# Another order of the convolution units, norms of q and k spread through DRAM, and part of the last depthwise convolution on TensorE

## The chip, the cores and the metric

The kernel runs on one core of a Trainium2 chip: TensorE (PE), VectorE (DVE), ScalarE (ACT), GpSimd (POOL) and SyncE (SP), each with its own in-order instruction stream, and the DMA engines that they feed. The time is the device time of one execution in microseconds; a kernel's time is the median of its runs. All data are float32.

## The reference

The model has three layers: attention behind a hybrid of convolutions, a two-way state-space layer (mamba), and a mixture of experts. Only the first one bears on the change:

```python
x = x + conv_attn(_gn(x), W1, W3, W5, Wdw, Wproj, temperature)     # 1 x 64 x 64 x 256

def conv_attn(x, ...):
    qkv = concat([conv(xc, W1, 0), conv(xc, W3, 1), conv(xc, W5, 2)])   # q: 1x1, k: 3x3, v: 5x5
    qkv = conv(qkv, Wdw, 1, groups=3 * c)                               # 3x3 depthwise
    q, k, v = split(qkv)                  # 8 heads of 32 channels, 4096 pixels
    q, k = l2n(q), l2n(k)                 # t / max(sqrt(sum(t * t)), 1e-12)
    attn = softmax(einsum(q, k) * temperature)
    return conv(einsum(attn, v), Wproj, 0)
```

So q comes of a 1x1 convolution, k of a 3x3 and v of a 5x5 one, each followed by a depthwise 3x3 convolution; q and k are then divided by their norms over the 32 channels of a head.

## The kernel before

**Layout.** Channels lie on the 128 partitions, in two tiles of channels (t = 0, 1), pixels along the free axis. The image is worked in two halves of rows (half = 0, 1). One *unit* is a kind, a half and a tile, such as v10: kind v, half 1, tile 0. There are twelve: first k00, k01, k10, k11, then q00, v00, q10, v01, q01, v10, q11, v11.

**Products.** The convolutions k and v run as a Winograd scheme along the width. `weights` makes transformed weights on DVE (from raw weights that POOL loads into `wr`) and stores them to DRAM through POOL (`uk`, `uv`); SP loads them back as `u`. `inputs` makes the transformed image `v` from `xpad` on DVE. A unit of k has six products, one of v eight; each is a chain of matmuls of PE into one PSUM bank (`cv`, line 452, ten for v and six for k). A unit of q has four short products straight from `xpad` (line 444). `feed` (depth 3) issues products up to three ahead of those that DVE has taken, in the order of `units`; `product` hands out the next one.

**Main part of a unit.** `transform_out` takes the products in pairs: ACT copies one of a pair out of PSUM (`c`, L481), DVE adds and subtracts (L275, `out_t`) and sums into a padded image `pad` (L272); `sides` (ACT, L504 and L505) writes the two side columns. For q, `evacuate` lets ACT copy the four products into `pad`.

**Depthwise part.** `depthwise` makes tap 0 on ACT (L524) for two blocks, then the other eight taps of each on DVE (L528), 128x1280 elements a tap in half 1 and 128x768 in half 0. It is a generator and runs a unit late: the taps of one unit are stepped beside the main part of the next. For v, `turn` then transposes 128x128 blocks on PE (L587), copies them on ACT (L589) and stores them to `vd` through POOL (L590).

**Norms.** For q and k the rows go onto `rows_left` in chunks of 512 pixels; a *round* takes three. `norm_sums` squares on ACT (L550) and sums over a head on PE into `ps` (L551), the sum standing on eight rows a head, 32 a chunk. `norm_inverse` takes the maximum on DVE (L558), the root on ACT (L559) and the reciprocal on DVE (L560) of 96x512, then spreads it to all channels on PE (L565). `norm_apply` multiplies on DVE (L275, `acc`), puts q into another order on ACT (L574) and stores to `qd` or `kd` through POOL (L578). Each of the three is started one tick after the one before, from the list `events`; `tick` is called once a group.

**Order.** The engines' order is the program's (a schedule written out by hand). The loop over the units runs `groups` times per unit: 3 for k, 4 for v, 1 for q. In each group it steps the main part, calls `feed` and `tick`, steps the depthwise part of the unit before (18 steps over the groups), then does `share[kind]` steps of the filler work (`step_fill`: weights and inputs of later units), and feeds again.

```python
for g in range(groups):
    step(main)
    feed()
    tick()
    for _ in range(-(-18 // groups)):
        step(before)
    for _ in range(share[kind]):
        step_fill()
    feed()
```

**Hand-over.** After the last unit, `before` (the taps of v11) is drained, and then the events that are left. `Early` loads weights of the next layer (`win`, `wx`, `wdt`) on SP's queue and makes the diagonals `taps` on DVE (L802) in its constructor; then the attention phase loads `wpj`, the first `q`, and `kS` and `vT` for both tiles (`load_kv`), before its first scores (L954) and exponentials (L961).

Of the kernel before, what the change touches and what calls it, by code (L numbers as in the profile page):

```python
# [14 lines left out]
FP = mybir.dt.float32  # L15
# [9 lines left out]
P = 128  # L25
# [148 lines left out]
def conv_phase(cx, xT, w1, w3, w5, temp, qd, kd, vd, uk, uv):  # L174
# [17 lines left out]
    with ExitStack() as ctx:  # L192
# [56 lines left out]
        for t in range(CT):  # L249
            x = tp.tile([P, 4, 32], FP, name="px", tag="t")  # L250
            nc.vector.tensor_scalar(
                x, heads[:, None, :].to_broadcast([P, 4, 32]), temp[:, t : t + 1], None, ALU.mult
            )
            y = one.tile([P, 4, 32], FP, name=f"px{t}")
            nc.vector.tensor_tensor(y, x, first_of[:, None, :].to_broadcast([P, 4, 32]), ALU.mult)
            ps = pms.tile([P, N], FP, name="ps", tag=f"ps{t}")
            nc.tensor.transpose(ps[:, 0:P], y.rearrange("p a b -> p (a b)"), cx.ident)
            pq = one.tile([P, P], FP, name=f"pick_q{t}")
            nc.vector.tensor_copy(pq, ps[:, 0:P])
            pick_q.append(pq)  # L260
# [149 lines left out]


        units = [("k", h, t) for h in range(2) for t in range(CT)]
        for i in range(4):
            units += [("q", i % 2, i // 2), ("v", i // 2, i % 2)]
        jobs = [
            (u, i) for u in units for i in (range(4) if u[0] == "q" else PTS[u[0]])
        ]
# [85 lines left out]
        def sides(pad, r0):  # L503
            nc.scalar.copy(pad[:, r0 : r0 + HR, 0, 1:TX], pad[:, r0 : r0 + HR, 4, 0 : TX - 1])  # L504
            nc.scalar.copy(pad[:, r0 : r0 + HR, 5, 0 : TX - 1], pad[:, r0 : r0 + HR, 1, 1:TX])  # L505

        def depthwise(kind, half, t, pad):

            row0, n = (LAG, H - LAG) if half else (0, LAG)
            ch = {"q": 0, "k": CT, "v": 2 * CT}[kind] + t  # L510
            dst = accp.tile([P, (H - LAG) * W], FP, name="acc", tag="acc")

            def piece(b, tap):
                dy, dx = divmod(tap, 3)
                m = n // 2
                return (
                    dst[:, m * W * b : m * W * (b + 1)].rearrange("p (h w) -> p h w", w=W),
                    pad[:, m * b + dy : m * b + dy + m, dx : dx + 4, :].rearrange("p h s j -> p h (s j)"),
                    wdw[:, 9 * ch + tap : 9 * ch + tap + 1],
                )  # L520

            for b in range(2):
                o, src, w_ap = piece(b, 0)
                nc.scalar.activation(o, src, AF.Copy, scale=w_ap)  # L524
            for b in range(2):
                for tap in range(1, 9):
                    o, src, w_ap = piece(b, tap)
                    nc.vector.scalar_tensor_tensor(o, src, w_ap, o, ALU.mult, ALU.add)  # L528
                    yield
                if kind == "v":  # L530
                    turn(dst, t, row0 * W // P, n * W // P // 2 * b, n * W // P // 2)
            if kind != "v":
                c0 = row0 // ROWS
                rows_left.extend((dst[:, N * j : N * j + N], kind, t, c0 + j) for j in range(n // ROWS))
                if not busy:
                    norm_sums()

        def norm_sums():  # L540

            chunks = rows_left[:3]
            del rows_left[:3]
            busy[:] = chunks
            if not chunks:
                return
            ps = pms.tile([P, N], FP, name="ps", tag="ps0")
            for j, (a, _, _, _) in enumerate(chunks):
                sq = tp.tile([P, N], FP, name="sq", tag="t")
                nc.scalar.activation(sq, a, AF.Square)  # L550
                nc.tensor.matmul(ps[32 * j : 32 * j + 32, :], heads, sq, start=True, stop=True)  # L551
            later(lambda: norm_inverse(chunks, ps))

        def norm_inverse(chunks, ps):

            n = 32 * len(chunks)
            rn = rp.tile([P, N], FP, name="rn", tag="rn")
            nc.vector.tensor_scalar(rn[0:n, :], ps[0:n, :], 1e-24, None, ALU.max)  # L558
            nc.scalar.activation(rn[0:n, :], rn[0:n, :], AF.Sqrt)  # L559
            nc.vector.reciprocal(rn[0:n, :], rn[0:n, :])  # L560
            back = []
            for j, (_, kind, t, _) in enumerate(chunks):
                back.append(pms.tile([P, N], FP, name="ps", tag=f"ps{j}"))
                r = slice(32 * j, 32 * j + 32)
                nc.tensor.matmul(back[j], (pick_q[t] if kind == "q" else pick)[r, :], rn[r, :], start=True, stop=True)  # L565
            later(lambda: norm_apply(chunks, back))

        def norm_apply(chunks, back):
            for (a, kind, t, c), ps in zip(chunks, back):
                plus(a, a, ps, ALU.mult)  # L570
                if kind == "q":

                    s = tp.tile([P, N], FP, name="qo", tag="t")
                    nc.scalar.copy(  # L574
                        s.rearrange("p (h j r) -> p h r j", j=TX, r=4), a.rearrange("p (h r j) -> p h r j", r=4, j=TX)
                    )
                    a = s
                nc.gpsimd.dma_start(out=(qd if kind == "q" else kd)[t][:, N * c : N * c + N], in_=a)  # L578
            norm_sums()
# [25 lines left out]
        with tc.manual_schedule(engines=ORDERED):  # L605
# [85 lines left out]
                return False  # L691


            share = {"k": 5, "q": 4, "v": 3}
            before = None
            for n, (kind, half, t) in enumerate(units):
                pad, r0 = pads[n % 2], 9 if half else 1
                edge = edges["q" if kind == "q" else t]
                if half:
                    nc.scalar.copy(pad[:, 0:9], edge)  # L700
                    nc.gpsimd.memset(pad[:, HR + 9, :, :], 0.0)
                else:
                    nc.gpsimd.memset(pad[:, 0, :, :], 0.0)
                if kind == "q":
                    def evacuate():
                        for i in range(4):
                            r = r0 + 16 * (i // 2)
                            nc.scalar.copy(
                                pad[:, r : r + 16, 1 + 2 * (i % 2) : 3 + 2 * (i % 2), :],
                                product().rearrange("p (h s j) -> p h s j", s=2, j=TX),  # L710
                            )
                        sides(pad, r0)
                        yield

                    main, groups = evacuate(), 1
                else:
                    main, groups = transform_out(kind, pad, r0), len(PTS[kind]) // 2
                for g in range(groups):
                    step(main)
                    feed()  # L720
                    tick()
                    for _ in range(-(-18 // groups)):
                        step(before)
                    for _ in range(share[kind]):
                        step_fill()
                    feed()
                drain(main)
                drain(before)
                if not half:
                    nc.scalar.copy(edge, pad[:, LAG : LAG + 9])  # L730
                before = depthwise(kind, half, t, pad)
            drain(before)
            while events:
                tick()
# [5 lines left out]
class Early:  # L740
# [3 lines left out]
    def __init__(self, cx, pool, w_in, w_x, w_dt):  # L744
        nc = self.nc = cx.nc
        self.cx, self.pool = cx, pool
        self.win = pool.tile([P, CT, 2 * DI], FP, name="win0")
        nc.sync.dma_start(out=self.win, in_=w_in[0])
        self.wx = pool.tile([P, ET, DR + 2 * DS], FP, name="wx0")
        nc.sync.dma_start(out=self.wx, in_=w_x[0])  # L750

        self.wdt = pool.tile([32 + DR, DI], FP, name="wdt")
        for d in range(2):
            nc.sync.dma_start(out=self.wdt[32 * d : 32 * d + DR, :], in_=w_dt[d])
        self.taps = pool.tile([P, ET * 4, P], FP, name="taps0")
        diagonals(cx, self.taps, 0)

    def new_u(self):
        return self.pool.tile([P, CT, N], FP, name="u", tag="u")
# [53 lines left out]
def attention_phase(cx, early, xT, wproj, qd, kd, vd, x1d, ud):  # L813
# [8 lines left out]
    with ExitStack() as ctx:  # L822
# [10 lines left out]
        kS = one.tile([P, CT, NT], FP, name="kS")  # L833
        vT = one.tile([P, NB, C], FP, name="vT")
        wpj = tl.tile([P, CT, C], FP, name="wpj")
        nc.sync.dma_start(out=wpj, in_=wproj)
        ones = tl.tile([P, 32], FP, name="ones")
        nc.vector.memset(ones, 1.0)

# [98 lines left out]

        last, due, turning, queue = None, None, [], []
        q_next = load_q(0)  # L940
        for t in range(CT):
            load_kv(t)
        for c in range(NCH):
            q_t = q_next
            if c + 1 < NCH:
# [1050 lines left out]
def kernel(  # L1996
# [55 lines left out]
    with tc.If(nc.values_load(beyond[0:1, 0:1]) > 0):  # L2052
        general_attention_phase(cx, xT, wproj, over, qd, qg, kd, vd, md, x1g, ug)
        with tc.tile_pool(name="early", bufs=1) as pool:
            early = Early(cx, pool, w_in, w_x, w_dt)
            with tc.tile_pool(name="g_psx", bufs=2, space=PSUM) as psx:
                drain(early.stage(ug, lambda: psx.tile([P, 2, N], FP, name="sx", tag="sx")))
            mamba_phase(cx, early, w_in, w_x, w_out, w_m1, w_m2, x1g, ug, bcg, dtg, x2g, u2g, usum)
# [93 lines left out]
```

## Time and profile before

| what | us |
|---|---|
| median of 3 runs (lowest, highest) | 4239.93 (4239.77, 4242.26) |
| the profiled execution, its time | 4233.11 |
| its span | 4231.3 |
| PE busy (share of the span) | 3603.2 (85%) |
| DVE busy | 3503.0 (83%) |
| ACT busy | 2675.6 (63%) |
| POOL busy | 1740.9 (41%) |
| granted clock of PE, mean | 0.918 |
| last `pad` of the last unit starts | 635.97 |
| first matmul of the scores | 703.54 |
| first exponential | 706.98 |
| PE busy in the attention, 703.5 to 1990 | 1269.96 of 1286.50 |

The profile is of one execution, and times in it are from the start of its span. A group of instructions is named by its line, its engine and its tiles, written as output<-inputs; the number in brackets behind a row is the idle time of the engine before it and what ended it. "x12" is twelve instructions or records; a float32 matmul of this kernel leaves two records.

### The profile page before, as it was taken

Reading aid. Unit: us, or ns where it says so; the run is one execution under the profiler, and the core shown is the slowest. Engines: PE = TensorE matmul, PEld = TensorE weight load, DVE = VectorE, ACT = ScalarE, POOL = GpSimd, SP = SyncE. Lnnn points to the kernel's source line nnn. Section 1 sums busy time; section 2 is a strip of 40 time slices with the busy share of each in tenths; the row PEclk is TensorE's granted clock in tenths of the full one; section 3 lists DMA queues with packets and bytes.
Section 4 is the critical chain, followed back from the end, with each engine's and each line's share of the span. In section 5 each row is a group of like instructions: output and inputs, shape, how many; then the busy total and the mean of one; then the engine's idle time right before and its main releaser. Section 6 shows DMA issues by size and latency. Waiting matters only on the chain. (4 is left out here: it accounts for less than half of the span.)

```text
span 4231.3 us, 43479 instructions
## 1 busy us (share of the span) xinstructions
PE 3603.2 (85%) x15080; PEld 1175.6 (28%) x15080; DVE 3503.0 (83%) x2898; ACT 2675.6 (63%) x4176; POOL 1740.9 (41%) x1132
## 2 busy tenths in 40 slices
PE   4769894999999999999788888878888888875798
PEld 2324341222222222222222222222222222321343
DVE  6997876888888888778899999999999999999211
ACT  1111224888788788777777778777787777774122
POOL 2210000000000000000888889888888888897000
PEclk9889996999999999999888999989899898977899
DMA  4422224000000000002333443433334433432121
GB/s 160 138 77 92 75 75 133 4 28 15 21 26 11 24 24 15 17 14 74 115 125 113 130 117 123 126 115 123 115 108 125 130 124 116 133 117 73 65 65 39
DMA packets 150531, 351.18 MB, mean 83 GB/s; under 512 B 35493, under 2 KB 44453, under 8 KB 150046
## 3 DMA queue, kind: packets, MB, share of 16 engines
q1 hardware_dynamic: 139214, 313.17, 23.4%
q0 software_dynamic: 11088, 35.14, 2.4%
q8 instruction: 120, 1.97, 0.2%
q14 instruction: 109, 0.89, 0.1%
HBM read 268.69 MB, written 79.56 MB: 82 GB/s over the span
## 5 line engine op out<-in xcount | busy, mean ns | idle before, releaser
L1677 POOL TENSOR_TENSOR dbx<-dtxr,b 128x1024 f32<-128x1024 f32 x512 | 1203.0, 2361 | 201.9 <-DVE da L1688 106.0
L961 ACT ACTIVATE e<-sc 128x1024 f32<-128x1024 f32 x1024 | 992.6, 1023 | 201.4 <-PE sc L954 160.3
L1688 DVE TENSOR_TENSOR_SCAN da<-da,state,dbx 128x1024 f32<-128x1024 f32 x432 | 1014.3, 2348 | 40.4 <-ACT state L1716 19.3
L882 DVE TENSOR_TENSOR s<-s,e 128x1024 f32<-128x1024 f32 x768 | 880.8, 1218 | 45.4 <-ACT e L961 44.9
L1667 ACT ACTIVATE da<-dtr,aneg 128x512 f32<-128x512 f32 x1024 | 708.0, 691 | 32.8 <-DMA dtr<-dtd 2.9
L954 PE MATMUL sc<-q,kS 32*128 32x512 f32 x4096 | 653.6, 643 | 19.5 <-DMA kS<-kd 13.0
L132 POOL TENSOR_TENSOR ln_few<-ln_few,minus_half 128x4 f32<-128x4 f32 x29 | 29.5, 1016 | 1414.2 <-DMA ln_few<-ln_row 1414.2
L1693 DVE TENSOR_TENSOR h<-da,c 128x1024 f32<-128x1024 f32 x432 | 529.2, 1225 | 32.6 <-DVE da L1688 0.4
L889 PE MATMUL av<-e,vT 128*32 128x512 f32 x4096 | 548.9, 607 | 3.7 <-ACT o L895 3.7
L452 PE MATMUL cv<-v,u 128*128 128x512 f32 x928 | 420.7, 614 | 58.8 <-DVE pad L272 21.2
L1725 PE MATMUL y<-h,sel 128*32 128x512 f32 x2048 | 378.7, 655 | 101.3 <-DVE h L1693 83.9
L954 PEld LDWEIGHTS sc<-q,kS 32*128 32x128 f32 x4096 | 211.6, 183 | 465.5 <-issue 244.3
L1251 PE MATMUL mm<-u,win 128*128 128x512 f32 x496 | 255.4, 663 | 80.9 <-ACT z L1362 34.3
L452 PEld LDWEIGHTS cv<-v,u 128*128 128x128 f32 x928 | 181.1, 197 | 294.6 <-issue 241.3
L528 DVE SCALAR_TENSOR_TENSOR acc<-pad,wdw_s,acc 128x768 f32<-128x768 f32 (+1 forms) x192 | 244.6, 1279 | 19.0 <-ACT acc L524 13.3
L1716 ACT COPY state<-da 128x2 f32<-128x2 f32 x431 | 68.1, 158 | 257.9 <-DVE h L1693 256.8
L1297 PE MATMUL mm<-xp,taps 128*128 128x512 f32 x480 | 213.6, 597 | 3.5 <-DVE m L1446 3.4
L882 DVE TENSOR_TENSOR s<-e 128x1024 f32<-128x1024 f32 x128 | 150.9, 1220 | 72.8 <-ACT e L961 72.6
L1688 DVE TENSOR_TENSOR_SCAN h<-da,state,dbx 128x1024 f32<-128x1024 f32 x80 | 187.5, 2343 | 16.5 <-ACT state L1716 7.0
L889 PEld LDWEIGHTS av<-e,vT 128*32 128x32 f32 x4096 | 81.3, 108 | 395.9 <-issue 378.3
L1698 POOL TENSOR_TENSOR h<-h,c 128x1024 f32<-128x1024 f32 x80 | 188.6, 2358 | 2.1 <-ACT state L1716 2.1
L1251 PEld LDWEIGHTS mm<-u,win 128*128 128x128 f32 x496 | 100.9, 212 | 236.5 <-issue 105.1
(347 smaller groups left out, 3821.3 us busy)
## 6 DMA issues: line engine op xcount, KB each, us to landing
dtr<-dtd SPq DMA_DIRECT2D x128, 512.0 KB
dtxr<-dtd SPq DMA_DIRECT2D x128, 512.0 KB
b<-bcd SPq DMA_DIRECT2D x64, 256.0 KB
c<-bcd SPq DMA_DIRECT2D x64, 256.0 KB
dtd<-dt SPq DMA_DIRECT2D x64, 256.0 KB
dtd<-few SPq DMA_DIRECT2D x64, 256.0 KB
u<-uv SPq DMA_DIRECT2D x24, 640.0 KB
u<-ud SPq DMA_DIRECT2D x16, 512.0 KB
```

The lines of the kernel that those rows point to most:

```text
L452: nc.tensor.matmul(rows4(ps), u[:, dy, P * ci : P * ci + P], v[:, dy : dy + HR, ci, :], start=dy + ci == 0, stop=dy == k - 1 and ci == CT - 1,
L528: nc.vector.scalar_tensor_tensor(o, src, w_ap, o, ALU.mult, ALU.add)
L882: nc.vector.tensor_tensor(z, x, y, ALU.add)
L889: nc.tensor.matmul(g.av[32 * h : 32 * h + 32, :], vT[:, kb, P * t + 32 * h : P * t + 32 * h + 32], es[h // 2][:, h % 2, :], start=kb == 0, ...
L954: nc.tensor.matmul(ps[h // 2][:, h % 2, :], kS[r, t, P * kb : P * kb + P], q_t[r, t, :], start=True, stop=True,)
L961: nc.scalar.activation(e, ps[i], AF.Exp)
L1251: nc.tensor.matmul(ps, win[d][:, t, P * e : P * e + P], u[:, t, ::-1] if d else u[:, t, :], start=t == 0, stop=t == CT - 1,)
L1667: nc.scalar.activation(da[:, v, :], dts[i, e, j][0][:, v, :], AF.Exp, scale=aneg[i % 2][:, a : a + 1])
L1677: nc.gpsimd.tensor_tensor(u, dts[i, e, j][1], bcs[i, k][0][:, None, :].to_broadcast([P, 2, N]), ALU.mult)
L1688: nc.vector.tensor_tensor_scan(das[n].rearrange("p v n -> p (v n)"), da.rearrange("p v n -> p (v n)"), u.rearrange("p v n -> p (v n)"), st ...
L1693: nc.vector.tensor_tensor(h, da, bcs[i, k][1][:, None, :].to_broadcast([P, 2, N]), ALU.mult)
L1725: nc.tensor.matmul(ys[i, e][32 * j : 32 * j + 32, :], cx.sel, hs[n + j // 2][:, j % 2, :], start=False, stop=k == SQ - 1,)
```

## The change

**Order of the units:** the last eight are now q00, v00, q10, v01, q01, q11, v10, v11.

**Norms:** four steps in place of three. `norm_sums` is itself put on the list of events where it was called at once. `norm_roots` takes the root on ACT straight from PSUM, writes one row a head to DRAM (`norm_rows`, a DMA that ACT issues) and has POOL load them spread over 128 partitions (`few`, at most 128x48). `norm_inverse` takes the maximum and the reciprocal of `few` on DVE, stores them (`norm_back`) and loads them broadcast to the eight rows a head of `rn`, both through POOL. `norm_apply` does the matmuls that spread to the channels (line 610 of the changed kernel) and at once the multiplications.

**Ticks:** `tick` is called twice a group, before and after the depthwise steps, so that each step of the norms comes half a group after the one before.

**Filler steps:** six steps and a `feed` ahead of the first unit's groups; in q units twelve steps ahead of the depthwise steps in place of four behind them.

**Last unit:** of v11, 16 of 40 rows are computed on PE (`products`): nine matmuls for eight rows, each with a diagonal of one tap's weights that ACT makes (`diagonal`). DVE's taps of that unit cover 24 rows.

**Loads:** `Early` loads in a method of its own, called after the keys and values of the first tile; `wpj` is loaded last.

```diff
-            y = one.tile([P, 4, 32], FP, name=f"px{t}")
+            y = tp.tile([P, 4, 32], FP, name="py", tag="t")
...
-        for i in range(4):
-            units += [("q", i % 2, i // 2), ("v", i // 2, i % 2)]
+        units += [("q", 0, 0), ("v", 0, 0), ("q", 1, 0), ("v", 0, 1), ("q", 0, 1), ("q", 1, 1), ("v", 1, 0), ("v", 1, 1)]
...
+        diag = one.tile([P, 9, P], FP, name="diag")
+
+        def diagonal(ch):
+            for tap in range(9):
+                w_ap = wdw[:, 9 * ch + tap : 9 * ch + tap + 1]
+                nc.scalar.activation(diag[:, tap, :], cx.ident, AF.Copy, scale=w_ap)
+
+        def products(pad, r, ps):
+
+            for tap in range(9):
+                dy, dx = divmod(tap, 3)
+                nc.tensor.matmul(
+                    ps.rearrange("p (h s j) -> p h s j", s=4, j=TX), diag[:, tap, :],
+                    pad[:, r + dy : r + dy + 8, dx : dx + 4, :], start=tap == 0, stop=tap == 8,
+                )
...
+            shared = 16 if (kind, half, t) == units[-1] else 0
+            mine = n - shared
...
-                m = n // 2
+                m = mine // 2
...
+            parts = [pcv.tile([P, N], FP, name="cv", tag="cv") for _ in range(shared // 8)]
+            for i, ps in enumerate(parts):
+                products(pad, mine + 8 * i, ps)
             for b in range(2):
...
-                    turn(dst, t, row0 * W // P, n * W // P // 2 * b, n * W // P // 2)
+                    m = mine * W // P // 2
+                    turn(dst, t, row0 * W // P, m * b, m)
+                if b == 0 and shared:
+                    for i, ps in enumerate(parts):
+                        nc.scalar.copy(dst[:, W * (mine + 8 * i) : W * (mine + 8 * i + 8)], ps)
+                    turn(dst, t, row0 * W // P, 2 * m, shared * W // P)
...
                 if not busy:
-                    norm_sums()
+                    busy.append(None)
+                    later(norm_sums)
...
-            later(lambda: norm_inverse(chunks, ps))
-
-        def norm_inverse(chunks, ps):
-
-            n = 32 * len(chunks)
+            later(lambda: norm_roots(chunks, ps))
+
+        def spread(rows):
+            return rows.rearrange("r n -> (r n)").rearrange("(p j) -> p j", p=P)
+
+        def norm_roots(chunks, ps):
+
+            k = 4 * len(chunks)
             rn = rp.tile([P, N], FP, name="rn", tag="rn")
-            nc.vector.tensor_scalar(rn[0:n, :], ps[0:n, :], 1e-24, None, ALU.max)
-            nc.scalar.activation(rn[0:n, :], rn[0:n, :], AF.Sqrt)
-            nc.vector.reciprocal(rn[0:n, :], rn[0:n, :])
+            nc.scalar.activation(rn[0 : 8 * k, :], ps[0 : 8 * k, :], AF.Sqrt)
+            rows = cx.rows.tile([12, N], FP, name="norm_rows", tag="norm_rows", bufs=2)
+            nc.scalar.dma_start(out=rows[0:k, :], in_=rn[0 : 8 * k : 8, :])
+            few = rp.tile([P, 48], FP, name="few", tag="few")
+            nc.gpsimd.dma_start(out=few[:, 0 : 4 * k], in_=spread(rows[0:k, :]))
+            later(lambda: norm_inverse(chunks, rn, few))
+
+        def norm_inverse(chunks, rn, few):
+
+            k = 4 * len(chunks)
+            f = few[:, 0 : 4 * k]
+            nc.vector.tensor_scalar(f, f, 1e-12, None, ALU.max)
+            nc.vector.reciprocal(f, f)
+            back = cx.rows.tile([12, N], FP, name="norm_back", tag="norm_back", bufs=2)
+            nc.gpsimd.dma_start(out=spread(back[0:k, :]), in_=f)
+            nc.gpsimd.dma_start(out=rn[0 : 8 * k, :], in_=back[0:k, None, :].to_broadcast([k, 8, N]))
+            later(lambda: norm_apply(chunks, rn))
+
+        def norm_apply(chunks, rn):
             back = []
             for j, (_, kind, t, _) in enumerate(chunks):
                 back.append(pms.tile([P, N], FP, name="ps", tag=f"ps{j}"))
                 r = slice(32 * j, 32 * j + 32)
                 nc.tensor.matmul(back[j], (pick_q[t] if kind == "q" else pick)[r, :], rn[r, :], start=True, stop=True)
-            later(lambda: norm_apply(chunks, back))
-
-        def norm_apply(chunks, back):
             for (a, kind, t, c), ps in zip(chunks, back):
                 plus(a, a, ps, ALU.mult)
...
-            share = {"k": 5, "q": 4, "v": 3}
+            share = {"k": 5, "q": 0, "v": 3}
...
+                if n == 0:
+                    feed()
+                    for _ in range(6):
+                        step_fill()
                 for g in range(groups):
                     step(main)
                     feed()
                     tick()
+
+                    for _ in range(12 if kind == "q" else 0):
+                        step_fill()
                     for _ in range(-(-18 // groups)):
                         step(before)
+                    tick()
                     for _ in range(share[kind]):
                         step_fill()
                     feed()
...
                 before = depthwise(kind, half, t, pad)
+                if n == len(units) - 2:
+                    diagonal(2 * CT + units[-1][2])
...
+    def load(self):
+        nc, (w_in, w_x, w_dt) = self.nc, self.sources
         nc.sync.dma_start(out=self.win, in_=w_in[0])
-        self.wx = pool.tile([P, ET, DR + 2 * DS], FP, name="wx0")
         nc.sync.dma_start(out=self.wx, in_=w_x[0])
...
         q_next = load_q(0)
-        for t in range(CT):
-            load_kv(t)
+        load_kv(0)
+        early.load()
+        load_kv(1)
+        nc.sync.dma_start(out=wpj, in_=wproj)
```

More of the change, by code (lines that the diff above doesn't have):

```diff
@@ L747, in __init__ @@
         self.win = pool.tile([P, CT, 2 * DI], FP, name="win0")
+        self.wx = pool.tile([P, ET, DR + 2 * DS], FP, name="wx0")
+        self.wdt = pool.tile([32 + DR, DI], FP, name="wdt")
+        self.taps = pool.tile([P, ET * 4, P], FP, name="taps0")
+        self.sources = w_in, w_x, w_dt
+    def load(self):
+        nc, (w_in, w_x, w_dt) = self.nc, self.sources
         nc.sync.dma_start(out=self.win, in_=w_in[0])
-        self.wx = pool.tile([P, ET, DR + 2 * DS], FP, name="wx0")
         nc.sync.dma_start(out=self.wx, in_=w_x[0])
-        self.wdt = pool.tile([32 + DR, DI], FP, name="wdt")
         for d in range(2):
             nc.sync.dma_start(out=self.wdt[32 * d : 32 * d + DR, :], in_=w_dt[d])
-        self.taps = pool.tile([P, ET * 4, P], FP, name="taps0")
-        diagonals(cx, self.taps, 0)
+        diagonals(self.cx, self.taps, 0)
     def new_u(self):
@@ L835, in attention_phase @@
         wpj = tl.tile([P, CT, C], FP, name="wpj")
-        nc.sync.dma_start(out=wpj, in_=wproj)
         ones = tl.tile([P, 32], FP, name="ones")
@@ L2055 @@
             early = Early(cx, pool, w_in, w_x, w_dt)
+            early.load()
             with tc.tile_pool(name="g_psx", bufs=2, space=PSUM) as psx:
```

## The prediction

> **What bounds the kernel now.** The change touches the conv stage (span 0 to 636.7), the hand-over to attention (to the first Exp at 706.98) and nothing later, so I read first the busy time by stretch: the k units, q00 with v00's start, the other q and v units, the hand-over. Columns: stretch, length, then busy time of PE, PEld, DVE, ACT and POOL, and the granted clock.
>
> ```profile
> 41.33:272.50 231.17, 147.84 (x319) 61.57 (x318) 195.34 (x302) 21.49 (x32) 52.10 (x93) 0.82 0.37 121
> 272.50:397.30 124.80, 119.70 (x301) 49.39 (x301) 97.61 (x90) 29.32 (x48) 7.17 (x16) 0.98 0.24 82
> 397.30:636.70 239.40, 217.34 (x524) 91.93 (x522) 191.72 (x174) 51.10 (x74) 13.22 (x28) 0.94 0.21 73
> 636.70:703.50 66.80, 14.48 (x40) 5.26 (x40) 40.50 (x44) 15.29 (x22) 5.97 (x11) 0.55 0.26 88
> ```
>
> The k units are DVE's (195 of 231), the v units PE's (119.7 of 124.8, then 217 of 239), and the last 66.8 us are nobody's: a chain. Then the idle ahead of DVE, from its timeline and the table of waits:
>
> ```profile
> 51.83 1.29 DVE L275 TENSOR_TENSOR out_t<-cv,c 128x512 f32<-128x512 f32 x2 [10.49 <-ACT c L481]
> 71.13 1.29 DVE L275 TENSOR_TENSOR out_t<-cv,c 128x512 f32<-128x512 f32 x2 [7.02 <-ACT c L481]
> 80.95 0.43 DVE L275 TENSOR_TENSOR wx<-wr 128x256 f32<-128x256 f32 x1 [2.49 <-DMA wr<-in_w]
> 105.88 1.29 DVE L275 TENSOR_TENSOR out_t<-cv,c 128x512 f32<-128x512 f32 x2 [10.54 <-ACT c L481]
> ...
> DVE rn L560 <- ACT rn L559: 15.3, 12, 4.9
> DVE acc L275 <- PE ps L565: 12.3, 4, 5.0
> ```
>
> At the start DVE waits 30.5 us (the four idles) for products whose inputs it has not made yet. Last, the timeline of the hand-over:
>
> ```profile
> 635.97 0.69 DVE L272 SCALAR_TENSOR_TENSOR pad<-cv,out_t 128x512 f32<-128x512 f32 x1 [4.20 <-PE cv L452]
> ...
> 640.64 25.30 DVE L528 SCALAR_TENSOR_TENSOR acc<-pad,wdw_s,acc 128x1280 f32<-128x1280 f32 x16 [2.52 <-ACT acc L524]
> 665.86 0.68 DVE L558 TENSOR_SCALAR rn<-ps 96x512 f32<-96x512 f32 x1
> 671.47 3.35 DVE L560 RECIPROCAL rn<-rn 96x512 f32<-96x512 f32 x1 [4.93 <-ACT rn L559]
> 690.55 1.28 DVE L275 TENSOR_TENSOR acc<-acc,ps 128x512 f32<-128x512 f32 x2 [2.22 <-PE ps L565]
> 690.70 0.33 SPq L748 DMA_DIRECT2D win<-in_w_in  x1
> 703.54 3.78 PE L954 MATMUL sc<-q,kS 32*128 32x512 f32 x12 [12.99 <-DMA kS<-kd]
> 706.98 1.94 ACT L961 ACTIVATE e<-sc 128x1024 f32<-128x1024 f32 x2
> ```
>
> From the last pad (end 636.66) to the first Exp 70.3 us pass: 25.3 of taps, 24.6 of two rounds of norms (665.86 to 690.55), then loads.
>
> **k units: −26.** Six fill steps are put ahead of the first unit. A step of inputs is six operations of 128x1152 at 1.35 us (8 us), of weights six of 0.42 us; they fill waits instead of following them: of 30.5 us I leave 3 (−27.5). Two norm rounds fall here; each gives up on DVE the max (0.68), the wait for ACT's root (0.70) and the reciprocal (3.35): 4.73, twice is −9.5. The new max and reciprocal are 128x48; DVE's reciprocal of 128x16 takes 0.25 and of 96x512 3.35, and I take 0.4 for the two together (+0.8 for both rounds; in proportion to columns it could be 0.7 each). New on the path: the back product (L610) and the multiplication that needs it (DVE, plus) now stand in one tick. PE runs in order, so plus waits for the product queued ahead: once a cold k product less DVE's cover (+6), once less (+1.7). POOL issues three more DMAs a round at 0.54 and waits in its queue for DVE's reciprocal; the wr loads behind it start later (+2). Sum −27.5 −9.5 +0.8 +6 +1.7 +2 = −26.5; between −15 (half the fills' gain is taken by waits behind the six steps, since the first pad comes after them) and −37 (nothing new waits).
>
> **v00: +3.** Its first out_t work comes later by one step of fills set between pairs; PE has products queued meanwhile.
>
> **v01: +6.5.** Two rounds less, −9.4, but the back product stands behind two products of v (8.64 each: 20 records of 0.432), and plus on DVE behind it. Laid out in the order that the changed program issues, DVE waits 12.9 in sum, and PE, whose three finished products nobody takes meanwhile, stands 3: 67.7 − 9.4 + 12.9 + 3 = 74.2. Lower end −9.4 (no wait), upper +16 (two whole products more).
>
> **q01 and q11 back to back: +16.** Now each q unit has a v unit after it, so PE multiplies for v while DVE does 16 taps. After the change v01's taps (16 of 1.01 us) lie beside q01 with only q11's four products (1.88 each, 7.5 in all) to run, and q01's taps beside q11's. The two units, 30.7 in all, stood at 6.8 + 8.0 before. The 12 fill steps in q find the fills nearly used up, and cost nothing there; if they did not, they would be in the k units' sum.
>
> **v10 and v11: +30.** Now 156.9 for the two. PE needs 138 for 16 products of 8.64 and some 15 for q and turns; idle that the order makes: 4.7 and 9.5 (first multiplication behind three queued products, 26 us of PE, then 16 taps that must pass before products are consumed), 4, 5.5, and 7 at the end, 31 in all; cold restarts add about 2.8 each, of which I count one, since the others fall on idle that is there anyway. 138 + 15 + 31 + 3 = 187. Bounds: +8 where DVE keeps up, +40 with all the restarts. What a restart costs is in the timeline of PE for k: twelve records behind an idle of 7.04 take 8.09, a pair of products without one 10.57, or 5.29 each.
>
> ```profile
> 166.25 10.57 PE L452 MATMUL cv<-v,u 128*128 128x512 f32 x24
> 183.86 8.09 PE L452 MATMUL cv<-v,u 128*128 128x512 f32 x12 [7.04 <-DVE out_t L275]
> ```
>
> The Trainium skill ("TensorE: Matmul & The Clock Gate", Part 1) says an idle window of some 3.4 us halves the clock until about as long has been worked. That speaks against this change, which makes five idles above that length where before had two; by the rule each costs about 1.7 us, an estimate from its figures, and the sum would be 1 us lower than by the row's 2.8.
>
> **The trip through DRAM** (root on ACT, rows out on ACT's queue, few in, reciprocal, back and broadcast on POOL's) isn't in the trace; the nearest row is attention's denominator, same shape, on SP's queue:
>
> ```profile
> 868.56 1.12 SPq L920 DMA_DIRECT2D den_rows<-rs  x4
> 870.72 0.35 SPq L923 DMA_DIRECT2D den_few<-den_rows  x1
> 873.79 0.34 SPq L927 DMA_DIRECT2D den_back<-den_few  x1
> 875.23 0.55 SPq L928 DMA_DIRECT2D rs<-den_back  x1
> ...
> 879.97 0.69 DVE L933 TENSOR_TENSOR oT<-o,rs 128x512 f32<-128x512 f32 x1 [5.13 <-DMA rs<-den_back]
> ```
>
> From 868.56 to the reciprocal (873.5) 5.0, from there to the use 6.4: 11.4. Each leg has half a group: in v 8.6 us (one product), in k about 6 to 10. I cost it at nothing: cover is 8.6 against 5.0 and 6.4. Without cover a round costs what is over, bounds 0 and 5 us. On ACT an issue (0.33 on SP, 0.54 on POOL) delays the c copies behind it, and on POOL kd and qd stores stand behind DVE's plus as they did before; 1 us in all is within the sum's error.
>
> **Hand-over: −34.** v11 now comes last, q's norms end a unit earlier, so both rounds (24.6) leave. Its last 16 rows go to PE: 18 matmuls with a diagonal, 36 records of 0.432 = 15.6; DVE's 16 taps shrink to 128x768, 1.01 each, 16.7 with hand-offs. Laid out from the last pad's end: sides, v10's last turn and the first tap on ACT 7.2; taps to 23.9; PE's products, cold at first, to 24.4; q's load issued at 24.5 with win, wx and wdt no longer ahead of it; kS landed at 32 (7.5 later, against 8.75 from issue at 694.76 to 703.51); scores, table load 1.28, first Exp at 36. 70.3 − 36 = 34.3. Bounds −24 (kS takes 10 more behind v11's turns) and −40. The nine diagonals on ACT (a 128x512 copy 0.58, a 128x2 copy 0.16; 1.4 to 5.2 in all) lie in ACT's idle, 188 of 239 us. Loads of win, wx, wdt and wpj go behind the first keys; attention's PE, 1270 of 1286 busy, doesn't wait for them.
>
> **The rest.** Sums of squares start half a group later through the same list of due steps, with nothing waiting for them there; the small tile px moved to another pool lies before 41 us. Both at nothing: if the later sums push the last round past a unit's end, it costs one round's wait, 4.7, within the bounds of that unit.
>
> **Sum:** −26.5 +3 +6.5 +16 +30 −34 = −5 on the profiled execution of 4233.1 (span 4231.3 and 1.8 around it), so 4228; the median of the runs lies 6.8 above that execution, so I put 4235 (4239.9 − 5).
>
> **Rivals.** *Nothing waits behind products* (faster): where PE is less far ahead than laid out, L610 is soon reached and the v terms fall to −9.4 and +8: −26.5 +3 −9.4 +16 +8 −34 = −43, so 4197. For it: DVE's waits on L565 are only 12.3 in 4 times now. Against: PE is at 0.96 of v00's stretch, so the three products ahead are usually there. *The trip overruns its half groups* (slower): about eight rounds lie under q and v units; if POOL's queue makes a leg 4 us longer than 8.6, PE stands at L610 and DVE with it, 8 x 4 = 32, so 4235 + 32 = 4267. It decides from a leg of 8.6 us. For it: POOL's loads of wr land a median 5.0 and more after issue; against: den's legs of 5.0 and 6.4. *Only DVE's work counts*: ten rounds of 4.73 outside the hand-over and −34, about 4159, as if DVE were the bound everywhere; against it the PE shares of the first view.
>
> **Numbers.** The laid-out sum 0.40 (4222 to 4250), nothing waits 0.30 (4185 to 4209), overrun 0.28 (4253 to 4281), the last 0.02. A measurement tells 0.2% (8.5 us) from no change. Of the first case 0.12 is faster, 0.18 the same, 0.10 slower; the second and last faster but for 0.02; the third slower: faster 0.42, same 0.20, slower 0.38. Range 4188 to 4276, which leaves out the outer quarter of the two rivals and the last case, some 0.17.
>
> **What would show it.** Right: DVE idle before 110 under 10 us; DVE idle "acc <- PE" at L610's multiplication, 10 us and more in v01 and v10; PE idle above 20 us from v01 to the last pad; last pad near 668 and Exp 36 after it. Wrong: PE waiting for DMA at L610; last pad before 640; a wait for win or wx in the hand-over.

## The result, and the profile after

The changed kernel takes 4237.49 us (median of 12 runs, 4230.59 to 4247.83), the kernel before on the same occasions 4241.51 (12 runs, 4232.83 to 4251.54): a ratio over these runs of 0.9994, 95% interval 0.9985 to 1.0003. The forecast was 4235, 5 us less than before; measured are 4 less, which these runs can't tell from nothing.

The median says little about the parts, but the end of the convolutions is sharp in a profile. From here on a unit ends at the second copy of `sides` (its start), and the stage at the first exponential. Times are from each profile:

| stretch | before | changed | difference | forecast |
|---|---|---|---|---|
| k units, to their end | 273.1 | 245.6 | −27.6 | −26.5 |
| q00 | 10.6 | 13.3 | +2.7 | none |
| v00 | 72.5 | 76.4 | +3.9 | +3 |
| q10 | 10.6 | 14.2 | +3.5 | none |
| v01 | 98.8 | 107.9 | +9.1 | +6.5 |
| q01 and q11 | 15.4 | 33.4 | +18.0 | +16 |
| v10 and v11 | 156.2 | 183.1 | +26.9 | +30 |
| last unit's end to first exponential | 69.8 | 35.2 | −34.6 | −34 |
| first exponential at | 706.98 | 708.94 | +2.0 | −5 |

The remainder, which the change doesn't touch but for the later loads, lasted 3524.3 us in the profile of before and 3536.4 in that of the changed kernel; in the profiles of the experiments it lies between 3526 and 3535. So a single time is uncertain by about that, and the first exponential is the better measure. How far it repeats shows in e3 and e6 below, whose programs are the same as the changed kernel's to the end of the k units and, in e6, up to the last unit. The k units end at 243.94 and 242.12 there, at 245.56 here; the last unit of e6 ends at 673.83, here at 673.78. So single places differ by 3.4 us between like programs, and differences of that size between two profiles say nothing.

Busy time by stretch: first the q and v units of the kernel before, then the k units, the q and v units and the hand-over of the changed kernel (length; PE, PEld, DVE, ACT, POOL; granted clock; DMA).

```profile
273.12:637.20 364.08, 336.42 (x824) 141.21 (x822) 289.21 (x263) 80.41 (x124) 20.29 (x42) 0.96 0.22 76
```

```profile
41.33:245.56 204.23, 146.37 (x320) 60.81 (x319) 189.26 (x301) 22.15 (x34) 55.38 (x99) 0.84 0.44 142
245.56:673.78 428.22, 352.63 (x834) 145.36 (x832) 266.27 (x272) 89.69 (x141) 37.62 (x73) 0.90 0.21 70
673.78:708.94 35.16, 26.53 (x78) 12.53 (x78) 20.35 (x34) 9.15 (x17) 5.41 (x10) 0.79 0.38 129
```

DVE has the k units nearly to itself (189 of 204). In the q and v units neither engine is full: PE stands (is idle) 75.6 of 428.2 us, where before it stood 27.7 of 364.1, and its work is also slower, 352.6 busy (834 records) for 336.4 (824 records), at a clock of 0.90 for 0.96. The table of waits names what is new:

```profile
DVE acc L275 <- PE ps L610: 124.4, 9, 32.6
...
PE ps L610 <- DMA rn<-norm_back: 14.7, 4, 5.3
```

DVE waits 124 us in 9 times for the back product (L610); PE itself waits 14.7 for the rows that come back from DRAM. One such round, in v11, from the timeline of all engines:

```profile
610.60 34.60 PE L451 MATMUL cv<-v,u 128*128 128x512 f32 x80
...
621.58 0.45 DVE L599 RECIPROCAL few<-few 128x48 f32<-128x48 f32 x1
...
624.42 1.29 DVE L272 SCALAR_TENSOR_TENSOR out_t<-out_t 128x512 f32<-128x512 f32 x2
626.06 0.59 POOL L602 DMA_DIRECT2D rn<-norm_back  x1 [3.19 <-DMA norm_back<-few]
645.12 1.13 PE L610 MATMUL ps<-rn,pick_q 32*128 32x512 f32 x6
646.28 1.88 DVE L275 TENSOR_TENSOR acc<-acc,ps 128x512 f32<-128x512 f32 x3 [20.57 <-PE ps L610]
...
649.75 1.16 ACT L576 ACTIVATE sq<-acc 128x512 f32<-128x512 f32 x2
650.45 2.43 PE L577 MATMUL ps<-sq,heads 128*32 128x512 f32 x4 [4.19 <-ACT sq L576]
```

DVE is done at 625.7 and stands to 646.3. PE isn't idle meanwhile: it works off the four products that stand ahead of the back product (80 records, 34.6 us). The trip is the smaller part of this wait: its last transfer is issued at 626.06, and these transfers land a median of 3.0 us after issue. Then the roles change: nobody has taken the products, so nothing is queued, and PE stands 4.2 us for the next round's squares, which ACT makes after DVE's multiplication. The hand-over:

```profile
672.53 0.68 DVE L272 SCALAR_TENSOR_TENSOR pad<-cv,out_t 128x512 f32<-128x512 f32 x1
...
678.85 16.80 PE L517 MATMUL cv<-pad,diag 128*128 128x512 f32 x36
...
680.34 16.71 DVE L548 SCALAR_TENSOR_TENSOR acc<-pad,wdw_s,acc 128x768 f32<-128x768 f32 x16 [5.66 <-ACT acc L541]
...
697.20 0.80 SPq L906 DMA_DIRECT2D q<-qd  x2
...
705.42 3.78 PE L1011 MATMUL sc<-q,kS 32*128 32x512 f32 x12 [2.50 <-DMA kS<-kd]
...
708.94 2.85 ACT L1018 ACTIVATE e<-sc 128x1024 f32<-128x1024 f32 x3
```

Taps on DVE and products on PE end within 1.4 us of each other, no round of norms is left, and from the load of q to the first exponential 11.7 us pass.

### The profile page after: what moved, and what is told of

It is laid out like the page before. It is cut to its first block, busy times and chain, and to the rows that moved or that the text cites. A ratio compares the mean times of both kernels' runs of the same rounds, so it can differ in the third digit from the quotient of the medians.

```text
span 4245.3 us, 43641 instructions
## 1 busy us (share of the span) xinstructions
PE 3628.3 (85%) x15116; PEld 1186.4 (28%) x15116; DVE 3453.7 (81%) x2898; ACT 2677.3 (63%) x4187; POOL 1760.2 (41%) x1168
## 5 line engine op out<-in xcount | busy, mean ns | idle before, releaser
L1724 ACT ACTIVATE da<-dtr,aneg 128x512 f32<-128x512 f32 x1024 | 708.1, 691 | 32.6 <-DMA dtr<-dtd 3.0
L1011 PE MATMUL sc<-q,kS 32*128 32x512 f32 x4096 | 653.1, 643 | 10.2 <-ACT e L1018 7.5
L451 PE MATMUL cv<-v,u 128*128 128x512 f32 x928 | 418.1, 611 | 51.6 <-DVE pad L272 26.9
```

What stands on the lines that cost most here:

```text
L451: nc.tensor.matmul(rows4(ps), u[:, dy, P * ci : P * ci + P], v[:, dy : dy + HR, ci, :], start=dy + ci == 0, stop=dy == k - 1 and ci == CT - 1,
L1011: nc.tensor.matmul(ps[h // 2][:, h % 2, :], kS[r, t, P * kb : P * kb + P], q_t[r, t, :], start=True, stop=True,)
L1724: nc.scalar.activation(da[:, v, :], dts[i, e, j][0][:, v, :], AF.Exp, scale=aneg[i % 2][:, a : a + 1])
```

## The experiments

Each is the changed kernel with one edit, unless it says otherwise. The first exponential stands first, then the time of a single run or the ratio to the kernel before.

**e1, the multiplication a tick later.**

```diff
+            later(lambda: norm_scale(chunks, back))
+        def norm_scale(chunks, back):
             for (a, kind, t, c), ps in zip(chunks, back):
```

> The changed kernel with the multiplication by the spread norms put one tick after the back product (L610) in place of in the same tick. Theory W (what the change gives back in the v units is DVE waiting for a back product that stands behind queued products): DVE's waits for it fall from 124 us to under 40, the v units that hold rounds (v01, v10) get shorter by 25 us together, first exponential near 684 in place of 708.9, time 20 to 30 us below the changed kernel. Theory O (what is given back comes of q01 and q11 standing back to back, so PE stands in one place and is ahead in the next): the waits of DVE only move to the next row that needs a product, first exponential within 5 us of 708.9.

First exponential 695.06, 13.9 earlier; ratio 0.9969 (0.9959 to 0.998). DVE's waits for the back product fell only to 96 us. A gain, half as large as W said, with most of the waits still there.

**e2, tick ahead of feed.**

```diff
                     step(main)
-                    feed()
                     tick()
+                    feed()
```

> The changed kernel with the first tick of a group ahead of the feed in place of behind it, so that a back product of that tick stands ahead of the product that this feed queues. Theory W: about half of the 124 us of waits go, first exponential near 695. Theory O: first exponential within 5 us of 708.9.

695.98, waits 98 us, one time of 4226.3: as W said for the end, but the waits fell by a fifth and not by half.

**e3, the order of units of before.**

```diff
-("q", 0, 1), ("q", 1, 1), ("v", 1, 0), ("v", 1, 1)]
+("q", 0, 1), ("v", 1, 0), ("q", 1, 1), ("v", 1, 1)]
```

> The changed kernel with the order of units of before (q11 between v10 and v11). Theory O: the q units take 15 us in place of 33 and the v units lose their surplus too, last pad near 640; the hand-over gets longer by the rounds of q11 that now fall into it, 10 to 20 us; first exponential near 690. Theory W: DVE's waits for the back product stay near 120 us, v01, v10 and v11 keep most of their surplus, first exponential 700 to 712.

Last unit's end 650.9 in place of 673.8, so the order costs 22.9 us in the units; hand-over 72.1 in place of 35.2, since q11's rounds fall into it. First exponential 723.06, time 4259.42: in all the new order is worth 14 us. Neither theory had the hand-over's 37, and both have the end too early. The surplus of v01 stayed (107.9 us), as W said; the waits fell to 96 us, where W had about 120.

**e4, norms on DVE as before**, without the trip through DRAM; `norm_apply` as changed.

```diff
-            later(lambda: norm_roots(chunks, ps))
+            later(lambda: norm_inverse(chunks, ps))
...
+            nc.vector.tensor_scalar(rn[0:n, :], ps[0:n, :], 1e-24, None, ALU.max)
+            nc.scalar.activation(rn[0:n, :], rn[0:n, :], AF.Sqrt)
+            nc.vector.reciprocal(rn[0:n, :], rn[0:n, :])
+            later(lambda: norm_apply(chunks, rn))
```

> The changed kernel with the norms' maximum, root and reciprocal on 96x512 as before, without the trip through DRAM (ticks, order and all else as changed). Theory W: the trip is hidden, and the 4.1 us of DVE a round that it saves count only where DVE has no wait: k units 8 us longer, v and q stage within 8 us, first exponential at 715 to 725. Theory T (the trip is itself a cost, by its waits of PE for rn and by POOL's queue): first exponential below 700.

697.02 and one time of 4226.07: the end came 12 us earlier, below 700 as theory T said, where W expected it 6 to 16 later. The k units ended at 245.25 against 245.56, so the 4 us that a round saves on DVE bought nothing there that these profiles can tell, and in the q and v units DVE was 34 us busier and yet 11 us sooner done. DVE's waits were 55 us in 8 times, the longest 10.3. Here W is incomplete; whether T's reason is the right one, e9 and e10 take up.

**e5, no filler steps ahead of the first unit.**

```diff
-                if n == 0:
-                    feed()
-                    for _ in range(6):
-                        step_fill()
```

> The changed kernel without the six filler steps ahead of the first unit. Theory F (the 27.6 us that the k units gained are these steps' alone, since the rounds of norms there come out even): the k units end near 270 in place of 246, first exponential near 733. Theory R (the cheaper rounds on DVE are part of it): the k units end below 262, first exponential below 725.

k units end at 263.8, first exponential 728.86, between the two theories: the steps are worth 18 us with the changed norms. With the norms of before (e8) the k units end at 246.2, 27 before the kernel before; so the two parts overlap there: either alone gives 9 (norms, e11) or 27 (fills), both together 27.6.

**e6, all of v11's taps on DVE.**

```diff
-            shared = 16 if (kind, half, t) == units[-1] else 0
+            shared = 0
...
-                if n == len(units) - 2:
-                    diagonal(2 * CT + units[-1][2])
```

> The changed kernel with all 40 rows of v11's depthwise part on DVE (no products with a diagonal on PE, and no diagonals made). Theory S (DVE's taps set the hand-over): 16 taps of 1.546 in place of 1.012, last pad to first exponential 44 in place of 35.2. Theory L (loads and turns set it): under 39.

Hand-over 42.3 us in place of 35.2, so S, nearly: sharing is worth 7.1.

**e7, e4 with the multiplication a tick later:** the edits of e4 and e1 together.

> The changed kernel with the norms on DVE as before (no trip through DRAM) and the multiplication a tick after the back product. Theory W (DVE waits where the multiplication stands in one tick with the back product): DVE's waits for the back product, 55 us in the kernel without the trip and with both in one tick, fall under 20, first exponential 682 to 692 against 697 there. Theory O (the order of q units sets the v units): first exponential 694 to 700.

678.16; ratio 0.9925 (0.9908 to 0.9941); waits 24.9. The end is earlier than W said; the waits stayed somewhat above its 20.

**e8, norms wholly as before**: `norm_sums` to `norm_apply` from the kernel before, and

```diff
-                    busy.append(None)
-                    later(norm_sums)
+                    norm_sums()
...
                         step(before)
-                    tick()
```

> The changed kernel with the whole handling of norms as before: three steps, a round's sums at once, the back product a tick ahead of the multiplication, one tick a group. Order of units, filler steps, shared last unit and loads stay as changed. Theory W: v01 and v10 come back to about 99 and 76 us, DVE's waits for the back product under 20 us, first exponential 665 to 690, time 20 to 40 us below the changed kernel. Theory O: v10 stays above 100 us, first exponential above 695.

672.43, 36.5 us ahead of the changed kernel; 4205.1 us, ratio to before 0.9918 (0.9901 to 0.9934): faster than both by far more than they differ. Busy time by stretch:

```profile
41.33:246.17 204.84, 146.37 (x320) 60.81 (x319) 195.80 (x301) 22.11 (x33) 52.19 (x93) 0.84 0.43 138
246.17:636.55 390.38, 342.44 (x834) 142.07 (x832) 298.80 (x271) 88.44 (x139) 20.27 (x42) 0.93 0.21 71
636.55:672.43 35.88, 26.15 (x78) 12.42 (x78) 21.66 (x37) 11.09 (x18) 5.96 (x11) 0.83 0.37 123
```

Against the changed kernel the q and v units are 37.8 us shorter, though DVE does 32.5 us more in them: PE stands 47.9 in place of 75.6, and 834 records, as many, take 10.2 less at the higher clock. v01 took 98.8 us, as before; v10 took 77.4, near the 76.2 of before, not 111.2; DVE's waits for the back product are 14.4. All of this is W's. v11 is the exception: 81.3 us, where the changed kernel has 71.9.

**e9 and e10, on which of a group's two ticks the back product falls.** In e4 all of them fall on the second tick, after the taps; in the changed kernel, whose round has a step more, they alternate. e9 keeps the changed kernel to the second, e10 keeps e4 to the first.

```diff
-            later(lambda: norm_apply(chunks, rn))
+            later(lambda: norm_apply(chunks, rn), 2 - clock[0] % 2)     # e9
+            later(lambda: norm_apply(chunks, rn), 1 + clock[0] % 2)     # e10, in e4
```

> The changed kernel, trip through DRAM and all, with one thing other: back product and multiplication are started at the second tick of a group only (after the taps), never at the first (right after a feed, with the group's two products just queued). Theory P (what a round costs is the tick on which its back product falls): no wait of DVE for a back product over 12 us, in sum under 60 in place of 124, first exponential 690 to 702, unless rounds that come later reach into the hand-over. Theory T (the trip itself costs): waits in sum over 90, first exponential 704 or later.

> The kernel without the trip through DRAM (e4), with back product and multiplication at the first tick of a group only. Theory P: waits of 13 to 33 us come back without any trip, in sum over 110 in place of 55, first exponential 706 or later in place of 697. Theory T: waits under 70 in sum, first exponential within 4 us of 697.

e10: first exponential 739.77, 42.8 us later than e4, time 4273.38. The table of waits of e4, and then of e10:

```profile
DVE acc L275 <- PE ps L594: 55.0, 8, 10.3
```

```profile
DVE acc L275 <- PE ps L594: 112.0, 10, 32.4
```

Same arithmetic, no trip, the other tick: twice the waits. e9: 693.77, 15 us ahead of the changed kernel, time 4227.1, and with the trip no later than e4 without it (697.02). So the trip isn't what separates the changed kernel from e4; the tick is. But P's sum was wrong: e9's waits stayed at 105 us, as T had them, three of them of 14 to 24. DVE's waits alone don't measure the loss. PE's idle goes with it: 58.1 us in e9's q and v units and 63.6 in e4's, against 75.6 in the changed kernel's and 96.6 in e10's. This is in part so by construction, since a stretch is PE's busy time and its idle. The q and v units of e9, e4 and e10:

```profile
240.30:654.38 414.08, 355.95 (x830) 147.06 (x828) 265.36 (x270) 87.43 (x139) 36.50 (x71) 0.90 0.21 72
```

```profile
245.25:662.25 417.00, 353.42 (x834) 145.99 (x832) 300.00 (x272) 89.56 (x141) 21.29 (x44) 0.90 0.20 68
```

```profile
247.67:704.66 456.99, 360.43 (x834) 148.27 (x832) 300.08 (x272) 89.33 (x141) 21.29 (x44) 0.87 0.18 62
```

**e11, the kernel before with the norm part alone:** the reverse of e8, put into the kernel before (four steps, sums by `later`, a second `tick` after the depthwise steps).

> The kernel before with the norm part of the change alone (four steps with the trip through DRAM, the multiplication in the tick of the back product, sums a tick later, two ticks a group), all else as before. From e8, where the changed kernel without this part has its first exponential 36.5 us earlier, theory W expects it to cost 25 to 45 us here too where the parts add up: first exponential 732 to 752 in place of 707, k units within 5 us of 273, time 4265 to 4290. Theory D (in the order of before, with a v unit after every q unit, DVE's relief of 4 us a round is worth its waits): first exponential below 712.

748.83, 41.9 later than before; 4286.52 us, ratio 1.0113 (1.0088 to 1.0139). The k units ended 8.7 earlier, more than W allowed; the q and v units took 37.2 more and the hand-over 13.3 more. What the trip costs where nothing covers it stands in the timeline of the hand-over there:

```profile
699.35 0.59 ACT L562 ACTIVATE rn<-ps 96x512 f32<-96x512 f32 x1
699.97 0.71 ACTq L564 DMA_DIRECT2D norm_rows<-rn  x1
...
705.39 0.19 DVE L573 TENSOR_SCALAR few<-few 128x48 f32<-128x48 f32 x1 [10.90 <-DMA few<-norm_rows]
705.61 0.45 DVE L574 RECIPROCAL few<-few 128x48 f32<-128x48 f32 x1
...
712.11 2.08 PE L585 MATMUL ps<-rn,pick_q 32*128 32x512 f32 x6 [13.12 <-DMA rn<-norm_back]
714.19 1.88 DVE L275 TENSOR_TENSOR acc<-acc,ps 128x512 f32<-128x512 f32 x3 [8.12 <-PE ps L585]
```

DVE waits 10.9 us to the maximum and 8.1 more to the use, 19 in sum, but not all of that is the trip. Of the first wait 5.5 us pass before the first transfer is issued at 699.97, since ACT takes the root only behind its copies for v11's turns. The trip itself takes 5.6 us from that issue to the reciprocal and 6.5 from there to the spreading product, 12.1 in all; the product adds 2.1.

## Why the prediction came out right

The likeliest case, a wash of large terms, is what happened, and the terms are those of the table: none of the six is off by more than 3.1 us. So close a fit is in part luck: like programs differ by up to 3.4 us at one place, and two terms, v00 and v01, have the right size with a wrong reason or a wrong part.

**k units (−26.5; −27.6).** DVE's four idles of 30.5 us shrank to 1.19 and 4.06, both for raw weights. The forecast's balance inside the term, −27.5 for the fills and about +1 for the norms, fits e8 (−27.0 without the new norms) and e4 (0.3 between the norms), within those 3.4 us. It doesn't follow that the norms would give nothing without the fills: e11 has 8.7.

**v00, v01 (+3, +6.5; +3.9, +9.1).** v00's term had a step of fills as its reason. e8 keeps the fills, and its v00 takes 72.5 us, as before; so the norms lengthen v00. DVE's waits stand there, and in q10 and v01:

```profile
301.89 1.88 DVE L275 TENSOR_TENSOR acc<-acc,ps 128x512 f32<-128x512 f32 x3 [12.78 <-PE ps L610]
...
322.23 1.88 DVE L275 TENSOR_TENSOR acc<-acc,ps 128x512 f32<-128x512 f32 x3 [4.07 <-PE ps L610]
...
341.81 1.88 DVE L275 TENSOR_TENSOR acc<-acc,ps 128x512 f32<-128x512 f32 x3 [7.09 <-PE ps L610]
...
379.09 0.69 DVE L275 TENSOR_TENSOR acc<-acc,ps 128x512 f32<-128x512 f32 x1 [11.53 <-PE ps L610]
...
418.69 1.88 DVE L275 TENSOR_TENSOR acc<-acc,ps 128x512 f32<-128x512 f32 x3 [13.95 <-PE ps L610]
```

In v01 the mechanism is the forecast's, but the waits are 11.5 and 14.0 us, 25.5 in sum, twice the 12.9 of its sum. One of its readings was off, too: the stretch from 272.5 to 397.3, which it calls q00 with v00's start, holds q00, v00, q10 and the first 30 us of v01. Its 67.7 us for v01 fit the part behind 397.3; the whole unit takes 98.8.

**q01 and q11 (+16; +18.0).** As laid out, PE is short of products beside the two sets of taps:

```profile
456.25 3.51 PE L443 MATMUL cv<-xpad,wq 128*128 128x512 f32 x4 [15.10 <-DVE pad L272]
...
475.18 1.12 PE L629 MATMUL tr<-ident,acc 128*128 128x128 f32 x4 [7.37 <-DVE acc L548]
...
483.58 1.09 PE L629 MATMUL tr<-ident,acc 128*128 128x128 f32 x4 [5.92 <-DVE few L598]
```

In e8, with the norms of before, the two units take 37.6 us, so this is the order's.

**v10 and v11 (+30; +26.9).** The size holds, and so does the place, though the two units part: v10 takes 35.0 us more, v11 8.1 less. With the 20.6 us shown above for v11, the waits are 32.6, 21.5 and 20.6:

```profile
516.66 1.88 DVE L275 TENSOR_TENSOR acc<-acc,ps 128x512 f32<-128x512 f32 x3 [32.64 <-PE ps L610]
...
590.41 1.88 DVE L275 TENSOR_TENSOR acc<-acc,ps 128x512 f32<-128x512 f32 x3 [21.49 <-PE ps L610]
```

The forecast's sum had 138 and 15 us of work, 3 for a cold restart and 31 idle. PE was busy 156.55 of the 183.10 us from 490.68 to 673.78 and idle 26.55, so the work and the restart came out, and the idle was put some 4 us too large.

Over all q and v units PE's busy time grew by 16.2 us, with ten records more; against e8, which has as many records, it is 10.2 more, at a clock of 0.90 for 0.93. PE's idles above 3.4 us are eight in these units of the changed kernel, four in e8 and two before. The Trainium skill ("TensorE: Matmul & The Clock Gate", Part 1) has an idle window of about 3.4 us halve the clock until PE has been busy for about as long. By that rule, as an estimate from its figures, the changed kernel's idles cost some 10 us more than those of before and some 7 more than e8's; the measured 16.2 and 10.2 are of that order and above it.

**Hand-over (−34; −34.6).** As laid out, to the microsecond: first exponential 35.7 after the last pad's end, for 36. e6 gives 7.1 of it to the shared rows. e3 has 37 for the order, but with the changed norms, whose rounds lengthen a hand-over that holds them (by 13.3 us in e11); so the two don't add up to 34.6. What the later loads give was not run alone.

**What was left out.** q00 and q10 each take 3 us more, 6.2 in all. In q10 DVE waits 7.1 us for the back product (341.81 above). "The 12 fill steps in q ... cost nothing there" failed in so far as one of the two units' differences may be theirs; e8, which keeps those steps, has q10 at 10.6 again and q00 at 12.3, so it is the norms for q10, and open for q00. With these 6 the sum is +1, and the profile says +2. They are in the last pad, too: it starts at 672.5, where the forecast had it near 668.

**The trip.** It was costed at nothing, from attention's denominator (11.4 us, and half groups of 8.6 as cover). The forecast calls that the same shape; it has 4 rows of 512 (`den_few` is 128x16), a full round of norms 12 (`few` is 128x48). The time is nearly the same: 12.1 us in e11. But the cover wasn't always there. Three times in the q and v units PE had run out of products 1.0 to 4.9 us after the reciprocal's start, and the back product could begin 5.9 to 7.6 us after it. PE waited 14.7 us in 4 times, which the forecast had named as a sign of being wrong. Yet e9 against e4 shows no cost of the trip where the tick is the same; what separates the changed kernel from e4 is the step that the trip adds to a round, which puts every second back product on the first tick. The forecast had the waits of v01, v10 and v11 in its terms.

**The rivals.** "Nothing waits behind products" (4197) failed as a forecast, but e7 and e8 come within 14 and 8 us of it (4211 and 4205) when the norms are started otherwise. "The trip overruns" (4267) didn't happen: where PE waited for the trip in the q and v units, its second leg took 7.6 us at most, below the 8.6 from which that case decides. "Only DVE's work counts" fell with e4 and e8: DVE does about 33 us more in the q and v units, and they end sooner.

**What the wash hides.** Order, fills, shared rows and loads together are worth 34.5 us (before to e8), and the norms cost 36.5 (e8 to changed; 41.9 alone, e11). Within the norms, putting the multiplication into the tick of the back product costs 13.9 us with the trip (e1) and 18.9 without (e4 to e7). The two ticks and the later sums, left in e7, account for 5.7 (e7 to e8). The trip with its extra step accounts for 12 to 17 (changed to e4, e1 to e7); e9 with e10 show that the 12 come of the tick on which the back product falls. Why the trip still makes 17 between e1 and e7 was not taken apart further.

## What to carry to other kernels

An in-order engine that is kept several items ahead makes a small item queued behind them late for everyone: put it ahead of the feed, and let its user come a step later (13 and 14 us here, e2 and e1). Cheaper work for an engine gained nothing here in a stage that another engine bounds, and lost there because the cheaper form has one more step that must fall on the right place of the loop. Before taking a change that measures as nothing, undo its parts one at a time: here a gain of 34.5 us lay under a loss of 36.5.

## What was not expected of the hardware

A round trip through DRAM of 12 rows of 512 (rows out on ACT's queue, three transfers on POOL's) took 12.1 us in e11, from its first issue to the product that uses it, hardly more than the 11.4 of attention's trip with 4 rows on SP's queue: three times the bytes made little difference. And as many records of PE in the same units, 834, took between 342.4 us (e8, clock 0.93) and 360.4 (e10, clock 0.87). How many long idles there are doesn't settle it: the changed kernel and e10 both have eight above 3.4 us, with 352.6 and 360.4. What does was not run.
